# Sending one row of attention weights through DRAM instead of TensorE, and splitting the last block's feed-forward in two

## The chip, the cores and the metric

The kernel runs on one core of a Trainium2 chip, all in float32. The metric is device time in microseconds: the median of three runs, and beside it one profiled execution, from which all durations are taken. The engines are TensorE (PE; its weight loads are PEld), VectorE (DVE), ScalarE (ACT), GpSimd (POOL) and SyncE (SP), which here issues every DMA.

## The reference, cut to what matters

The input is x of shape (2, 4096, 256). First comes a recurrent mixing layer (a scan over 4096 tokens, then a group norm and a projection), added to x. Then come two layers of local attention and a gated feed-forward:

```
h = shift_token(x)                    # second half of the channels comes from the token before
q, k, v = split(h @ wqkv)             # 8 heads of 64
q, k = rotary(l2norm(q) * qs), rotary(l2norm(k) * ks)
# windows of 128 queries; keys: this window and the one before
mask = (i < j) | (i > j + 128)        # each query sees itself and the 128 tokens before it
o = softmax(q k^T * 8, masked) @ v
x = x + o @ wo
h = layernorm(shift_token(x)) * lg + lb
a, g = split(h @ w1 + b1)             # 682 each
x = x + (a * gelu(g)) @ w2 + b2
```

So each query sees 129 keys: 128 that can be laid out in 128 columns, and one more, the last key of the window before.

## The kernel before, in words

The work of the attention and feed-forward is cut into windows of 128 tokens, numbered n = 0 to 127, and blocks of four windows (512 tokens, number k): 2 sequences x 2 layers x 8 blocks. The recurrence of the first sequence runs ahead of them; that of the second runs beside the first windows.

A window with neighbours packs its 256 scores into 129 columns. Column 0 is the last key of the window before; columns 1 to 128 are the keys of this window, and where a query may not see its own window's key (a later one), the column holds the key of the window before that stands one place lower. Thus `pr[n]` is a tile of 128 queries x 8 heads x 129 weights. Column 0 is added onto column 1. `transpose_p(n, s)` transposes columns 1 to 128 of four heads each on TensorE into `ppt`, a PSUM bank. It copies them to `pT`, and multiplies them with the mask `backs` into `pB`, which keeps only the weights of keys of the window before. The mask leaves row 0 of `pB` empty, and column 0 of `pr`, turned into a row for each head, belongs there. In the kernel before, a ninth transposition (128 x 8 in, 8 x 128 out) brings this column to PSUM, a copy brings it to the small tile `last`, and a DMA writes `last` as row 0 of `pB`:

```
            pt = bank([P, W])
            nc.tensor.transpose(pt[:HEADS, :], pr[:, :, 0], ident)
            last = tile_of([P, W], "last", 2)[:HEADS]
            either(last, pt[:HEADS, :])
            nc.sync.dma_start(out=pBs[n][0:1], in_=last)
```

`values(n)` multiplies `pT` with the window's values `vt` and `pB` with `dv`, the difference between the values one window back and these (`vr`, the old values moved down by one row by DMA, minus `vt`, on POOL). It stands in one piece with `scores(n + 1)`, right behind its matmuls. Four of 128 windows start a sequence and have no window before (`lone`), so `pB` is made 124 times. There is one `pB` buffer.

After attention, `output` adds the projection by `wo` to x. `shift` moves half of the channels by one token with DMAs (tile `h`), and `normed` normalizes `h`. Before, `transpose_h(k)` transposes all four windows of a block when the last is there, and the feed-forward of the block follows over the next windows, in tiles of 512 tokens. `hidden` is one matmul pair over 128 columns of `w1`; `gate` and `remainders` copy gate tiles out of PSUM; `gelus` runs GELU over them as one unbroken piece on ScalarE; `value` multiplies the other half in; `down_ends` and `down` multiply by `w2`, one window at a time, and store. `fill(n, i)` places these steps into the windows that come after. For the last block no windows come after, and its feed-forward stands alone at the end.

No order is written by hand. Every call is only recorded, with a row (`plan.at`) as its priority; `order()` then simulates engines with fixed costs from `cost()` and puts out each engine's instructions in the order of planned starts. Among what can start first on an engine, the lowest row goes first. `either` lets the planner choose between ScalarE and VectorE for a copy. A DMA is planned to land `LAND` = 2500 ns plus its passes after its issue. PSUM has eight banks, which the planner hands out. All instructions are thus issued from line 524 (518 and 520 for scaling), so groups are told apart by their tiles. SP issues in order: when one DMA waits, those behind it wait too.

Of the kernel before, what the change touches and what calls it, by code (L numbers as in the profile page):

```python
# [15 lines left out]
P = 128  # L16
# [5 lines left out]
NM = 6  # L22
# [38 lines left out]
LEAN = 700  # L61
SLACK = 1.06
LOAD = 1283
LAND = 2500
TURN = {"row": 195, "col": 95, "full": 199}
SETS = {AF.Exp: 1, AF.Tanh: 1, AF.Gelu: 2, AF.Ln: 3}
# [15 lines left out]
class View:  # L82
# [51 lines left out]
    def to_broadcast(self, shape):  # L134
        return View(
            self.place,
            self.rows,
            np.broadcast_to(self.idx, shape[1:]),
            [*self.chain, ("to_broadcast", (shape,), {})],
        )  # L140

    def bitcast(self, dtype):
        return View(self.place, self.rows, self.idx, [*self.chain, ("bitcast", (dtype,), {})])
# [37 lines left out]
class Plan:  # L181
# [39 lines left out]
    def dram(self, shape, name):  # L221
        place = Place(int(np.prod(shape[1:])))
        place.outer = True
        place.real = self.dram_pool.tile([P, place.size], F32, tag=name, name=name)
        return self.view(place, 0, shape)

    def at(self, row):
# [74 lines left out]
    def cost(self, o):  # L302

        views = [*o.outs, *o.ins]
        n = max([v.idx.size for v in views] or [1])
        psum = any(v.place.psum for v in views)
        inside = sum(v.idx.size == n and not v.place.psum for v in o.ins)
        o.set, o.lock, o.half, o.passes, name, hold = None, False, "full", 0, o.name, None
        if o.eng == "tensor":
            trans = name == "transpose"  # L310
            left = o.args[1]
            move = o.args[2] if len(o.args) > 2 else o.args[1]
            cols = max(move.idx.size, left.idx.size) if not trans else P
            o.step = (1 if trans else 2) * (cols / 1.2 + (2 if cols >= 256 else 3))
            if not trans and left.shape[0] <= 64:
                o.half = "row"
            elif not trans and left.idx.size <= 64:
                o.half = "col"
            if o.half != "full":
                o.step /= 2  # L320
            o.time = o.step + 150
        elif o.eng == "vector":
            d = 150 + 1.04 * n
            if name == "tensor_tensor_reduce":
                d = 240 + 1.04 * n
            elif name == "tensor_tensor_scan":
                d, o.lock = 203 + 2.1 * n, True
            elif name == "scalar_tensor_tensor":
                d, o.lock = 200 + 1.05 * n, inside > 1
            elif name == "tensor_tensor":  # L330
                o.lock = inside > 1
            elif name == "tensor_scalar":
                d, o.lock = 155 + (1.27 if psum else 0.98) * n, not psum and n > 16
            elif name == "tensor_copy" and not psum:
                d, o.lock = 230 + 0.45 * n, n > 16
            elif name == "bn_aggr":
                d = 172
            elif name == "reciprocal":
                d = 147 + 4 * n
            o.step, o.time = max(d - 85, 60), d  # L340
        elif o.eng in ("scalar", "either"):
            d = (160 if psum else 195) + 0.83 * n
            if name == "scaled":
                d = 305 + 0.76 * n
            elif name == "activation":
                o.set = SETS.get(o.args[2])
                if o.args[2] == AF.Identity:
                    d = 365 + 0.87 * n
                elif isinstance(o.kw.get("bias"), View):
                    d += 85  # L350
            o.step, o.time = d - 100, d
            if "accum_out" in o.kw:
                o.time = d + 200
        elif o.eng == "gpsimd":
            o.lock = name != "memset"
            if name == "tensor_tensor":
                d = 430 + 156 * n if ALU.pow in o.args else 140 + 2.22 * n
            elif name == "tensor_scalar":
                d = 230 + 1.12 * n
            else:  # L360
                d = (100 if name == "memset" else 187) + 0.98 * n
            o.step, o.time = d, d
            hold = d if n > 64 else 100
        else:
            v = min(views, key=lambda v: v.shape[0] * v.idx.size)
            size = 4 * v.shape[0] * v.idx.size
            rows = max(v.shape[0] if v.shape[0] > 1 else v.shape[1] for v in views)
            ways = max(k for k in range(1, 17) if rows % k == 0)
            o.passes = size / 170 if ways == 16 else size / (25 * ways)
            inner = len(views) == 2 and not any(v.place.outer for v in views)  # L370
            o.step = 370 if not inner else 580 if ways in (1, 16) else 800
            o.time = LAND + o.passes
        o.hold = hold or o.time
# [154 lines left out]
def kernel(ctx: ExitStack, tc: tile.TileContext, a: dict, out: bass.AP):  # L528
# [581 lines left out]
    def softmax(n, g):  # L1110
# [42 lines left out]
        for m in range(2):  # L1153
            ph = prs[n][:, h0 + 2 * m, off:]
            nc.either.scaled(ph, ph, sums[:, m : m + 1])

    def transpose_p(n, s):


# [14 lines left out]
            ALU.mult,  # L1174
        )
        if s:
            pt = bank([P, W])
            nc.tensor.transpose(pt[:HEADS, :], pr[:, :, 0], ident)
            last = tile_of([P, W], "last", 2)[:HEADS]
            either(last, pt[:HEADS, :])  # L1180
            nc.sync.dma_start(out=pBs[n][0:1], in_=last)

    def values(n):

# [56 lines left out]
            nc.gpsimd.tensor_tensor(x[:, w, :], x[:, w, :], x1s[k][:, w, :], ALU.add)  # L1241
            plan.at(row)

    def transpose_h(k):
        l = blocks[k][0]
        h = hs.pop(k)
        hT = hTs[k] = tile_of([P, 2, T], "hT")
        for i in range(2):
            pt = bank([P, T])
            for w in range(NW):  # L1250
                nc.tensor.transpose(
                    pt[:, w * P : (w + 1) * P], h[:, w, i * P : (i + 1) * P], ident
                )
            g, bb = lnp[:, l, 0, i : i + 1], lnp[:, l, 1, i : i + 1]
            if i == 0:
                nc.scalar.activation(hT[:, i, :], pt, AF.Identity, bias=bb, scale=g)
            else:
                nc.vector.tensor_scalar(hT[:, i, :], pt, g, bb, ALU.mult, ALU.add)

    def hidden(k, c0, cols):  # L1260
        pm = bank([P, T])
        for i in range(2):
            nc.tensor.matmul(
                pm[:cols], w1[:, i, c0 : c0 + cols], hTs[k][:, i, :], start=(i == 0), stop=(i == 1)
            )
        return pm

    def gate(k, m):
        either(hm[:, m, :], hidden(k, m * P, P))

    def remainders(k):
        pm = hidden(k, G_LAST * P, HS)
        rems[k] = tile_of([P, NW // 2, P], "rem")
        for odd in range(2):
            rows = slice(64 * odd, 64 * odd + HR)
            nc.scalar.copy(ends[rows], of_half(pm[64:HS], odd))
            either(rems[k][rows], of_half(pm[:HR], odd))

    def of_half(t, odd):

        return t.rearrange("p (w two t) -> p w two t", two=2, t=P)[:, :, odd, :]

    def gelus(k):
        l = blocks[k][0]
        with piece():
            for m in range(NM - 1):
                g = hm[:, m, :]
                nc.scalar.activation(g, g, AF.Gelu, bias=b1[:, l, 1, m : m + 1])
            for odd in range(2):
                rows = slice(64 * odd, 64 * odd + HR)  # L1290
                g = ends[rows]
                nc.scalar.activation(g, g, AF.Gelu, bias=b1[rows, l, 1, NM - 1 : NM])

    def value(k, m):
        l = blocks[k][0]
        plan.early = k == NK - 1
        if m < NM - 1:
            src = hidden(k, G_LAST * P + HS + m * P, P)
            g = hm[:, m, :]
            nc.vector.scalar_tensor_tensor(g, src, b1[:, l, 0, m : m + 1], g, ALU.add, ALU.mult)  # L1300
        else:
            src = rems.pop(k)
            for odd in range(2):
                rows = slice(64 * odd, 64 * odd + HR)
                g = ends[rows]
                nc.vector.scalar_tensor_tensor(
                    g, src[rows], b1[rows, l, 0, m : m + 1], g, ALU.add, ALU.mult
                )
        plan.early = False

# [27 lines left out]
    def fill(n, i):  # L1338
# [4 lines left out]
            down(k, 2 * s)  # L1343
            down(k, 2 * s + 1)
        k = n // NW - 1
        if not 0 <= k < NK:
            return
        if s == 1:
            gate(k, i)
# [7 lines left out]
        elif s == 3 and i < 3:  # L1357
            value(k, i + 2)
            if i == 2:
                value(k, 5)  # L1360

# [80 lines left out]
    norms(0)  # L1444
    cosines(0)
    rotated(0)
    for n in range(NN + 6):
        k, w = divmod(n, NW)
        here, ahead, behind = n < NN, n + 1 < NN, 0 < n <= NN
        plan.at(n)  # L1450
# [44 lines left out]
        if behind:  # L1495
            output(n - 1)
            shift(n - 1)
            if here and n % (NB * NW) == 0:
                weights(n // (NB * NW) % L, "o")
        if w == 1 and 0 < k <= NK:  # L1500
            transpose_h(k - 1)
        if w == 2 and k + 1 < NK:
            transpose_x(k + 1)
# [17 lines left out]
        fill(n, 3)  # L1521
        if w < 2 and NW < n < NN and (n - NW - w) % (NB * NW) == 0:
            weights(n // (NB * NW) % L, "12"[w])
    with tc.manual_schedule():
        plan.give()

# [78 lines left out]
```

## Time and profile before

| | us |
|---|---|
| median of 3 runs | 2972.16 (2969.49 to 2972.76) |
| profiled execution, time | 2970.99 |
| profiled execution, span from first to last instruction | 2969.2 |
| TensorE busy | 2945.0 |
| VectorE busy | 2250.9 |
| ScalarE busy | 2018.8 |
| GpSimd busy | 1449.3 |
| DMA, share of 16 engines | 20.9% |

Busy time is the union of an engine's instructions. The durations of matmuls overlap in TensorE's pipeline, so what one costs is read from the distance between starts and not from its duration. A float32 matmul appears as two records in the trace, a transposition as one. "us to landing" of a DMA runs from its issue on SP until the last of its engines has counted up its semaphore.

### The profile page before, as it was taken

The numbers are of one execution on the slowest core, as the hardware profiler recorded it, in microseconds if no ns is written. First come the engines' busy times: TensorE is split into PE (matmuls) and PEld (weight loads), VectorE is DVE, ScalarE is ACT, GpSimd is POOL, SyncE is SP. The second block draws the span as 40 slices with busy tenths as digits, with TensorE's granted clock in tenths as the row PEclk, the third lists the DMA queues.
The fourth block names the chain that finished last, engine by engine and source line by source line (L and its number), as shares of the span: only waits on it lengthen the run. The fifth ranks groups of instructions, "written<-read, shape, count | busy, mean of one in ns | idle before, by whom it ended". The sixth has DMA issues, their size and how long they took to land.

```text
span 2969.2 us, 48964 instructions
## 1 busy us (share of the span) xinstructions
PE 2945.0 (99%) x15548; PEld 1913.7 (64%) x15548; DVE 2250.9 (76%) x5088; ACT 2018.8 (68%) x5359; POOL 1449.3 (49%) x1705
## 2 busy tenths in 40 slices
PE   9999999999999999999999999999999999999998
PEld 4476766666666666666666666666666666666665
DVE  7889999998866788786777677777676676767673
ACT  7887787778666777776666666666666666666663
POOL 2226654555554555445555444545454554555550
PEclk9999999999999999999999999999999999999999
DMA  2324322221121211111122221111112211111110
GB/s 85 114 78 133 115 69 87 75 82 53 60 65 54 83 48 53 56 59 55 52 77 79 74 68 48 61 58 61 55 44 70 70 57 49 58 55 54 47 40 27
DMA packets 185227, 195.09 MB, mean 66 GB/s; under 512 B 27812, under 2 KB 148484, under 8 KB 184456
## 3 DMA queue, kind: packets, MB, share of 16 engines
q1 hardware_dynamic: 184968, 191.96, 20.9%
q8 instruction: 123, 2.02, 0.3%
q14 instruction: 136, 1.11, 0.1%
HBM read 85.46 MB, written 39.85 MB: 42 GB/s over the span
## 4 chain that ended last, share of the span: by engine, by line
PE 92%; DVE 3%; ACT 3%; issue 1%; POOL 0%; DMA 0%; SPq 0%; POOLq 0%; ACTq 0%; DVEq 0%
PE bank L524 92%; ACT pr L524 1%; ACT L524 1%; DVE arena L524 1%; DVE bank L524 0%; ACT pr L520 0%; DVE sq L524 0%; DVE qk L524 0%; DVE h L524 0%; DVE nmx L524 0%; DVE hm L524 0%; DVE pB L524 0%; ACT arena L524 0%; ACT oT L524 0%; ACT hm L524 0%
## 5 line engine op out<-in xcount | busy, mean ns | idle before, releaser
L524 PE MATMUL bank<-wqkv,xT 128*128 128x512 f32 x1536 | 723.8, 596 | 0.5 <-ACT xT L524 0.5
L524 PE MATMUL bank<-hT,w 128*128 128x512 f32 (+1 forms) x1408 | 652.2, 595 | 0.0
L524 POOL TENSOR_TENSOR t<-qk,tab 128x256 f32<-128x256 f32 x512 | 383.6, 768 | 471.2 <-ACT qk L524 362.3
L524 ACT ACTIVATE pr<-bank,nmx 128x129 f32<-128x129 f32 (+1 forms) x1024 | 369.5, 379 | 147.8 <-DVE nmx L524 146.4
L524 PEld LDWEIGHTS bank<-hT,w 128*128 128x128 f32 (+1 forms) x1408 | 254.8, 189 | 260.9 <-issue 247.3
L524 PEld LDWEIGHTS bank<-wqkv,xT 128*128 128x128 f32 x1536 | 266.4, 191 | 210.9 <-issue 207.3
L524 POOL TENSOR_TENSOR rn<-rn,mhalf 128x16 f32<-128x16 f32 x128 | 391.7, 3060 | 8.8
L520 ACT ACTIVATE pr<-pr,sums 128x129 f32<-128x129 f32 (+1 forms) x948 | 334.1, 418 | 40.7 <-DVE pr L524 39.9
L524 DVE COPY_PREDICATED bank<-packs,bank 128x254 f32<-128x254 int32 x496 | 186.4, 420 | 229.8 <-PE bank L524 229.7
L524 PE MATMUL bank<-w,hm 128*128 128x256 f32 x1280 | 294.0, 381 | 0.0
L524 POOL TENSOR_TENSOR dv<-vr,vt 128x512 f32<-128x512 f32 x124 | 165.4, 1334 | 201.2 <-PE bank L524 188.1
L524 PEld LDWEIGHTS bank<-w,hm 128*128 128x128 f32 x1280 | 239.7, 190 | 35.0 <-issue 4.2
L524 ACT COPY qk<-bank 128x512 f32<-128x512 f32 x225 | 132.3, 588 | 170.5 <-PE bank L524 164.0
L524 PE MATMUL bank<-kT,qT 64*128 64x256 f32 (+1 forms) x2048 | 246.1, 380 | 0.4 <-ACT kT L524 0.4
L524 PE MATMUL bank<-wo,oT 128*128 128x256 f32 x1024 | 243.0, 380 | 1.4 <-ACT oT L524 1.3
L524 PEld LDWEIGHTS bank<-wo,oT 128*128 128x128 f32 x1024 | 193.4, 190 | 70.5 <-ACT oT L524 22.6
L524 PEld LDWEIGHTS bank<-kT,qT 64*128 64x128 f32 x2048 | 190.4, 187 | 68.8 <-issue 36.0
L524 DVE TENSOR_TENSOR pB<-bank,backs 128x512 f32<-128x512 f32 x248 | 170.0, 686 | 83.5 <-PE bank L524 56.7
L524 ACT ACTIVATION_READ_ACCUMULATOR pr<-bank,nmx 128x1 f32 x1024 | 221.8, 217 | 0.0
L524 ACT COPY hm<-bank 128x512 f32<-128x512 f32 x170 | 99.8, 587 | 174.1 <-PE bank L524 173.1
L524 PEld LDWEIGHTS bank<-mats,pr 128*128 128x128 f32 x1148 | 134.9, 135 | 115.7 <-issue 73.2
L524 PE MATMUL bank<-pT,vt 128*64 128x128 f32 x2048 | 203.3, 279 | 0.0
(159 smaller groups left out, 5625.3 us busy)
## 6 DMA issues: line engine op xcount, KB each, us to landing
vr<-vt SPq DMA_DIRECT2D x124, 224.0 KB
tab<-in_c_rot_dram SPq DMA_DIRECT2D x128, 128.0 KB
kT<-kT SPq DMA_DIRECT2D x64, 256.0 KB
z<-zd SPq DMA_DIRECT2D x16, 512.0 KB
x<-in_x_dram SPq DMA_DIRECT2D x16, 512.0 KB
x1d<-x SPq DMA_DIRECT2D x16, 512.0 KB
x<-x1d SPq DMA_DIRECT2D x16, 512.0 KB
h<-x SPq DMA_DIRECT2D x128, 64.0 KB
```

Source lines behind the costliest of these rows:

```text
L520: self.nc.scalar.activation(dst, src, AF.Copy, scale=scale)
L524: getattr(getattr(self.nc, o.eng), name)(*args, **kw)
```

## The change

First, column 0 of `pr` goes out as one DMA into a DRAM row, transposed by the access pattern (8 heads x 128 queries, one value at a time), and a second DMA brings the row back as row 0 of `pB`. Two DRAM rows take turns. The ninth transposition, its copy and `last` are gone. The planner gets a cost for such a transfer, `SINGLES` = 1500 ns of passes.

Second, the feed-forward of the last block is taken out of the loop over windows and done by a function of its own in two groups: each has two windows of 128 tokens, with all steps from `transpose_h` to `down`. Its matmuls of `hidden` have 256 columns instead of 512, so there are twice as many. The first group has a lower row number (128) than the second (130). The other blocks keep tiles of 512.

```diff
+SINGLES = 1500
...
+            if any(v.idx.size > 1 and v.idx.ravel()[1] != v.idx.ravel()[0] + 1 for v in views):
+                o.passes = SINGLES
...
+    fronts = [plan.dram([1, HEADS * W], f"front_{i}") for i in range(2)]
+
     def transpose_p(n, s):
...
         if s:
-            pt = bank([P, W])
-            nc.tensor.transpose(pt[:HEADS, :], pr[:, :, 0], ident)
-            last = tile_of([P, W], "last", 2)[:HEADS]
-            either(last, pt[:HEADS, :])
-            nc.sync.dma_start(out=pBs[n][0:1], in_=last)
+            row = fronts[n % 2]
+            nc.sync.dma_start(out=row.seen("o (h q) -> (o q) h", h=HEADS), in_=pr[:, :, 0])
+            nc.sync.dma_start(out=pBs[n][0:1].rearrange("o h q -> o (h q)"), in_=row)
...
-    def transpose_h(k):
+    def transpose_h(k, w0=0, w1=NW):
...
-    def hidden(k, c0, cols):
-        pm = bank([P, T])
+    def hidden(k, c0, cols, ts):
+        pm = bank([P, ts.stop - ts.start])
         for i in range(2):
             nc.tensor.matmul(
-                pm[:cols], w1[:, i, c0 : c0 + cols], hTs[k][:, i, :], start=(i == 0), stop=(i == 1)
+                pm[:cols], w1[:, i, c0 : c0 + cols], hTs[k][:, i, ts], start=(i == 0), stop=(i == 1)
             )
...
         k = n // NW - 1
-        if not 0 <= k < NK:
+        if not 0 <= k < NK - 1:
             return
...
+    def last_block():
+
+        k = NK - 1
+        for w in (0, 2):
+            plan.at(NN + w)
+            ts = slice(w * P, (w + 2) * P)
+            transpose_h(k, w, w + 2)
+            for m in range(NM - 1):
+                gate(k, m, ts)
+            remainders(k, ts)
+            gelus(k, ts)
+            for m in range(NM):
+                value(k, m, ts)
+            down_ends(NN + NW + w // 2)
+            down(k, w)
+            down(k, w + 1)
...
-    for n in range(NN + 6):
+    for n in range(NN + 2):
...
-        if w == 1 and 0 < k <= NK:
+        if w == 1 and 0 < k < NK:
             transpose_h(k - 1)
...
+    last_block()
```

More of the change, by code (lines that the diff above doesn't have):

```diff
@@ L140, in to_broadcast, with seen @@
         )
+    def seen(self, pattern, **sizes):
+        return View(self.place, self.rows, self.idx, [*self.chain, ("rearrange", (pattern,), sizes)])
     def bitcast(self, dtype):
@@ L223, in dram @@
         place.outer = True
-        place.real = self.dram_pool.tile([P, place.size], F32, tag=name, name=name)
+        place.real = self.dram_pool.tile([shape[0], place.size], F32, tag=name, name=name)
         return self.view(place, 0, shape)
@@ L1242, in shift @@
             plan.at(row)
-    def transpose_h(k):
+    def transpose_h(k, w0=0, w1=NW):
         l = blocks[k][0]
-        h = hs.pop(k)
-        hT = hTs[k] = tile_of([P, 2, T], "hT")
+        h = hs[k]
+        if w0 == 0:
+            hTs[k] = tile_of([P, 2, T], "hT")
+        hT = hTs[k][:, :, w0 * P : w1 * P]
         for i in range(2):
-            pt = bank([P, T])
-            for w in range(NW):
+            pt = bank([P, (w1 - w0) * P])
+            for w in range(w0, w1):
                 nc.tensor.transpose(
-                    pt[:, w * P : (w + 1) * P], h[:, w, i * P : (i + 1) * P], ident
+                    pt[:, (w - w0) * P : (w - w0 + 1) * P], h[:, w, i * P : (i + 1) * P], ident
                 )
@@ L1258, in transpose_h, with gate, halves, remainders @@
                 nc.vector.tensor_scalar(hT[:, i, :], pt, g, bb, ALU.mult, ALU.add)
-    def hidden(k, c0, cols):
-        pm = bank([P, T])
+    def hidden(k, c0, cols, ts):
+        pm = bank([P, ts.stop - ts.start])
         for i in range(2):
             nc.tensor.matmul(
-                pm[:cols], w1[:, i, c0 : c0 + cols], hTs[k][:, i, :], start=(i == 0), stop=(i == 1)
+                pm[:cols], w1[:, i, c0 : c0 + cols], hTs[k][:, i, ts], start=(i == 0), stop=(i == 1)
             )
         return pm
[L1268 to L1277, printed above, removed]
+    ALL = slice(0, T)
+    def gate(k, m, ts=ALL):
+        either(hm[:, m, ts], hidden(k, m * P, P, ts))
+    def halves(ts):
+        pairs = slice(ts.start // (2 * P), ts.stop // (2 * P))
+        return [(odd, slice(64 * odd, 64 * odd + HR), pairs) for odd in range(2)]
+    def remainders(k, ts=ALL):
+        pm = hidden(k, G_LAST * P, HS, ts)
+        if ts.start == 0:
+            rems[k] = tile_of([P, NW // 2, P], "rem")
+        for odd, rows, pairs in halves(ts):
+            nc.scalar.copy(ends[rows, pairs], of_half(pm[64:HS], odd))
+            either(rems[k][rows, pairs], of_half(pm[:HR], odd))
     def of_half(t, odd):
         return t.rearrange("p (w two t) -> p w two t", two=2, t=P)[:, :, odd, :]
-    def gelus(k):
+    def gelus(k, ts=ALL):
         l = blocks[k][0]
@@ L1286, in gelus, with value @@
             for m in range(NM - 1):
-                g = hm[:, m, :]
+                g = hm[:, m, ts]
                 nc.scalar.activation(g, g, AF.Gelu, bias=b1[:, l, 1, m : m + 1])
-            for odd in range(2):
-                rows = slice(64 * odd, 64 * odd + HR)
-                g = ends[rows]
+            for odd, rows, pairs in halves(ts):
+                g = ends[rows, pairs]
                 nc.scalar.activation(g, g, AF.Gelu, bias=b1[rows, l, 1, NM - 1 : NM])
-    def value(k, m):
+    def value(k, m, ts=ALL):
         l = blocks[k][0]
@@ L1297, in value @@
         if m < NM - 1:
-            src = hidden(k, G_LAST * P + HS + m * P, P)
-            g = hm[:, m, :]
+            src = hidden(k, G_LAST * P + HS + m * P, P, ts)
+            g = hm[:, m, ts]
             nc.vector.scalar_tensor_tensor(g, src, b1[:, l, 0, m : m + 1], g, ALU.add, ALU.mult)
         else:
[L1302 to L1305, printed above, removed]
+            for odd, rows, pairs in halves(ts):
+                g = ends[rows, pairs]
                 nc.vector.scalar_tensor_tensor(
-                    g, src[rows], b1[rows, l, 0, m : m + 1], g, ALU.add, ALU.mult
+                    g, rems[k][rows, pairs], b1[rows, l, 0, m : m + 1], g, ALU.add, ALU.mult
                 )
```

## The prediction

> **What bounds the kernel now.** I read the page's busy time first, then its chain, then TensorE's idle time by stretch, then the groups of the instructions that the change touches, and last the timeline of one window and of the end.
>
> ```profile
> PE 2945.0 (99%) x15548; PEld 1913.7 (64%) x15548; DVE 2250.9 (76%) x5088; ACT 2018.8 (68%) x5359; POOL 1449.3 (49%) x1705
> PE 92%; DVE 3%; ACT 3%; issue 1%; POOL 0%; DMA 0%; SPq 0%; POOLq 0%; ACTq 0%; DVEq 0%
> ```
>
> TensorE is busy 99% of the span, and 92% of the chain that ended last is its own work. The windows view says where the idle 24 us are:
>
> ```profile
> 300.00:600.00 300.00, 299.23 (x1657) 201.37 (x1654) 280.55 (x638) 234.98 (x615) 166.80 (x215) 1.00 0.27 85
> 2100.00:2400.00 300.00, 299.86 (x1628) 194.95 (x1626) 205.73 (x474) 188.16 (x534) 152.99 (x167) 1.00 0.21 64
> 2930.00:2935.00 5.00, 0.57 (x3) 0.57 (x4) 1.02 (x3) 0.06 (x1) 1.49 (x3) 0.93 0.08 28
> 2935.00:2940.00 5.00, 4.98 (x12) 2.36 (x11) 0.81 (x1) 1.31 (x2) 0.00 (x0) 0.73 0.01 3
> ```
>
> (The columns after the stretch are the busy us of PE, PEld, DVE, ACT and POOL, then the granted clock, the DMA share, GB/s.) Between 300 and 2890 us TensorE is busy 2586.45 of 2590, so there only less TensorE work shortens the kernel. At the end there is a real hole: 4.4 us idle in 2930 to 2935, after which the granted clock averages 0.73 for 5 us.
>
> The groups that the first edit removes:
>
> ```profile
> L524 PE MATMUL bank<-mats,pr 128*8 128x128 f32 x124 | 33.8, 273 | 0.0
> L524 ACT COPY last<-bank x97: 247/249/255, 272.9 to 2915.9; 8x128 f32<-8x128 f32 x97
> L524 DVE COPY last<-bank x27: 269/269/273, 355.7 to 2819.3; 8x128 f32<-8x128 f32 x27
> L524 SPq DMA_DIRECT2D pB<-last x124: 662/693/736, 273.8 to 2916.8; - x124
> ```
>
> And the timeline, one ninth transposition among its neighbours, then the end:
>
> ```profile
> 2900.13 0.27 PE L524 MATMUL bank<-mats,pr 128*8 128x128 f32 x1
> 2900.24 1.88 PE L524 MATMUL bank<-hT,w 128*128 128x512 f32 x4
> ...
> 2929.86 0.34 SPq L524
> 2930.25 1.96 DMA h<-x
> ...
> 2934.43 1.33 PE bank L524 x5
> ```
>
> The next matmul starts 0.11 us after the transposition, not 0.27: durations overlap in the pipeline. The last three lines are of the chain of waits: the last window's shifted rows are issued only behind an output store (2929.86), land 1.96 us later, and the normalized tile lets TensorE go on at 2934.43.
>
> **The change part by part. Sum against the profiled execution: span 2969.2 us, 2970.99 in all, 1.2 us under the median 2972.16.**
>
> *Removed: 124 transpositions.* How much each is worth is the main choice. The row's duration gives 124 x 0.273 = 33.8 us. The Trainium skill (TensorE: Matmul & The Clock Gate, Part 4: PE-mode transpose) also has about 275 ns for a transposition inside a kernel, and says that access latency is most of it; by that figure I would take 34 us off. But the sum must be made of steps: 0.11 us from start to start here, and eight query/key transpositions take 2901.96 to 2902.83, 0.109 each. So 124 x 0.109 = **13.5 us**, all of it in the stretch where TensorE is never idle. The changed program's instruction order has the same number of changes between full-array and half-array matmuls, so none of that is gained or lost.
>
> *Removed: the copies of the row out of PSUM.* 97 x 0.249 + 27 x 0.269 = 31.4 us of ScalarE and VectorE. Both have idle time (68% and 76% busy), so zero. From above: TensorE's whole idle time from 300 to 2890 is 3.5 us, and freeing a PSUM bank for some us per window can at most shorten that and small stalls that the busy time hides. From below: freed time reorders other work, which can also hurt. I take 0, ends -4 and +6 (gain).
>
> *Moved to DMA: per window a scatter of 128 x 8 single values into DRAM, then one 4 KB row back, in place of `pB<-last`.* Three things.
> (a) The landing. No row of before moves single values. The trace's completion events give, from issue to landing (medians): `pB<-last` 1.81 us (8 rows of 512 B), `kT<-kT` 2.71 (512 rows of 512 B, 32 for each of 16 engines), a 128 KB store `out_dram<-x` 1.86, a 128 KB load `tab<-in_c_rot_dram` 2.13. From the first two, (2.71 - 1.81)/32 = 28 ns for each 512-byte run. The scatter has 1024 runs, 64 for each engine: at most 64 x 28 = 1.8 us above 1.86, so 3.7; at least, with the 9 ns that a 4-byte packet takes in the packet records, 0.6 above, 2.4. Here a rule speaks against the change: the Trainium skill (DMA: Bandwidth & Descriptors, Rules for kernel authors) says that a last dimension with a stride becomes one descriptor per element, and warns off transposing by a rearranged access pattern, with a factor of 19. Nineteen times 1.81 is 34 us; with 13 us available in a window, 21 x 124 = 2600 us would be lost. I do not take it: the rows show that most of 1.81 us is fixed and that descriptors spread over engines, so only the 1024 count applies. I take 2.9 for the scatter and 2.1 for the row back: with wake-ups 5.2 us, against 0.25 + 1.81 + the transposition's place in the queue before.
> (b) Who waits for it. `values` of this window, which TensorE runs right behind the next window's scores. In the changed instruction order I summed steps (0.428 us per 512-column pass, half for 256, 0.109 per transposition, about 0.2 at each change of array half) from the eighth transposition to the first `pB` matmul: minimum 5.3, lowest 5% 7.1, median 8.8. The last weights are ready before that transposition: in the trace of before, from the last normalization of `pr` to the first `pB` matmul, median 13.1, lowest 5% 8.8, minimum 5.8. So 5.2 us fits in every window: **0 us**. The cover is the 8.8 us of feed-forward, projection and score matmuls; without it each late us would cost 124 us.
> (c) SP's queue. One more issue per window, 124 x 0.35 (a DRAM transfer such as `tab`) to 0.70 (`kT`): 43 to 87 us of a queue that already waits 654.6 us for POOL's `dv` alone. The second transfer waits for the first to land; in the changed order 1 to 9 other transfers stand between them (`vr`, `h`, `tab` mostly), each 0.35 to 0.85 us, so SP stands at most about 2 us in the 19 windows with only one between. Behind it then are `kT<-kT` (42 windows; the next scores wait for it) and `vr<-vt` (39; `dv` on POOL). Both are also late-bound on ScalarE's `kT` copy or on POOL, as before. I take 0, ends +3 and -10. Packets: 124 x 1024 x about 10 ns over 16 engines is 80 us each, 2.7% of the span, on top of 20.9%: hidden.
>
> *The last block in two groups.* Work is equal: 44 passes of 512 columns become 88 of 256, 0.214 each. Before, from the last `wo` matmul (ends 2927.2) to the last matmul (2966.2) is 39.0 us. In the changed order the first group's transpositions and four gates (0.4 + 3.4 us) stand before the last window's `values`, and 2.1 + 6.0 + 2.1 = 10.3 us of work (two `down`, seven hidden tiles) stand between the last `wo` matmul and the second group's transpositions. The last window's shift and norm takes 2927.2 to 2934.4 = 7.2 us, so the hole closes: +4.7, and with it the slow clock, 5 us at 0.73 = +1.35. What is late next: the first group's `down_ends` waits for the whole run of its gelus. After its remainder tile ScalarE needs two copies (0.4 each), a table load of 1.28, five gelus of half length (about 0.42) and two short ones, VectorE two products: about 6 us, over 3.4 us of TensorE work (one hidden tile, one `down`, four transpositions): -2.5. The second group's own gelus end with its last hidden tile, as before. Net of these and half-length evictions (about +1): **4.5 us**, ends 1.5 and 7.
>
> Sum: 13.5 + 4.5 = 18.0; 2971.0 - 18.0 = 2953.0 in the profile, and against the median **2954.2**.
>
> **Rivals.**
> *Rescheduling takes part of it back* (14%). The order is planned from estimated times, and each window shifts. For it: half-array turns and short stalls already hide some 0.6 us per window inside TensorE's busy time, as a window of 21.2 us holds 20.6 us of steps. Against: the steps between dependent instructions are nearly as in before. If it costs 0.05 us per window, 6 us, and the end gives 1.5: 2972.2 - 13.5 + 6 - 1.5 = 2963; with more, 2966, range 2960 to 2975.
> *The detour is late, and `values` waits* (11%): slower. Place: the first `pB` matmul of a window. Summing what is missing over the 124 windows with the second transfer and wake-ups at 2.2 us: nothing for a scatter of up to 4 us, 7 us at 5.0, 20 at 5.5, 33 at 6.0, 89 at 7.0. It decides from 5.5 us, or from some 1.5 us later as weights are ready before the eighth transposition. For it: no row shows 4-byte writes to DRAM, and SP issues in order. At 6.0 with no such credit: 2972.2 - 18 + 33 = 2987; up to 3043.
> *The freed bank and copies help too* (5%): 2954 - 10 = 2944.
> *The end does not split*: excluded by the changed instruction order, which shows the 256-column tiles before the last `values`.
>
> **How the numbers follow.** The main case, 70%, is 2954 with its own range 2946 to 2962 (the ends above: copies, SP, end). The range 2945 to 2968 adds over half of the first rival and part of the third. Left out: the slower case and the outer parts of the others, 2 in 10. A measurement of this kernel can tell 0.2%, 5.9 us, from no change: faster is below 2966.2. Faster: 0.70 + half of 0.14 + 0.05 = 0.82; same 0.07; slower 0.11.
>
> **What would show it.** Right: no `128*8` group, TensorE busy less by 13 to 17 us, no entry of PE waiting for DMA `pB<-front`, ScalarE's copies fewer by about 24 us, some 127,000 more packets, and at the end no TensorE hole over 3 us and a clock near 1.00. Wrong: PE or PEld waiting for `pB<-front`; SP waiting over 3 us for `front<-pr` in the median window; a landing of the scatter over 5 us; TensorE busy unchanged though the transpositions are gone (then stalls took their place); idle time in front of `w,ends` at the end of over 4 us.

## The result, and the profile after

The changed kernel takes 3551.26 us (median of 4 runs, 3546.63 to 3557.81) against 2971.36: a ratio of 1.1954, interval 1.1939 to 1.1968. It is 580 us slower, where 18 us faster was forecast. First the busy time of the page after, with the granted clock in its 40 slices and the DMA share:

```profile
span 3544.8 us, 48728 instructions
PE 3112.4 (88%) x15468; PEld 2014.1 (57%) x15468; DVE 2240.4 (63%) x5068; ACT 2013.8 (57%) x5281; POOL 1425.3 (40%) x1705
PEclk9999999989999999999999999999999999999999
DMA packets 312450, 195.59 MB, mean 55 GB/s; under 512 B 155904, under 2 KB 275584, under 8 KB 311680
q1 hardware_dynamic: 312192, 192.48, 24.4%
```

TensorE is now idle 3544.8 - 3112.4 = 432 us, before 24. Its busy time has grown by 167 us although 124 transpositions are gone. The mean granted clock of the execution is 0.948 instead of 0.998, and 5% of 3112 us is 156. So the loss is holes in TensorE's work, some 408 us, and slower running around them, the rest. There are 127,000 more DMA packets, as forecast, and the DMA engines' recorded share went from 20.9% to 24.4%: by this count they look mostly idle.

The windows view shows the same for the middle of the run (columns as in the prediction):

```profile
300.00:600.00 300.00, 259.99 (x1355) 176.41 (x1355) 223.82 (x502) 188.60 (x483) 138.98 (x175) 0.95 0.39 76
2100.00:2400.00 300.00, 270.45 (x1410) 176.25 (x1408) 190.18 (x441) 157.27 (x433) 121.09 (x148) 0.97 0.23 48
```

Who waited for a DMA, first before, then after (us in total, times, longest):

```profile
POOL x L524 <- DMA h<-x: 141.8, 41, 11.9
DVE st L524 <- DMA h<-x: 30.8, 27, 2.6
POOL tab L524 <- DMA tab<-in_c_rot_dram: 21.4, 21, 2.5
```

```profile
DVE st L531 <- DMA h<-x: 442.9, 72, 9.5
POOL x L531 <- DMA h<-x: 382.7, 42, 15.0
POOL tab L531 <- DMA tab<-in_c_rot_dram: 315.7, 53, 13.1
PE bank L531 <- DMA pB<-front: 177.1, 66, 5.5
```

The last line is the wait that a rival of the prediction named: `values` waits for the row. But the three above it are larger, and they wait for transfers that the change does not touch: the shifted half of `h`, from SBUF to SBUF, and the rotary table. The timeline of SP shows one window:

```profile
2120.61 0.49 SPq L531 DMA_DIRECT2D front<-pr  x1
2121.15 0.58 SPq L531 DMA_DIRECT2D vr<-vt  x1
2121.83 0.52 SPq L531 DMA_DIRECT2D xmd<-x  x1
2122.45 0.38 SPq L531 DMA_DIRECT2D tab<-in_c_rot_dram  x1
2132.22 0.24 SPq L531 DMA_DIRECT2D pB<-front  x1
```

The scatter is issued at 2120.61, and the second transfer can go only at 2132.22: the landing took over 11 us. In the waits of SP's queue:

```profile
SPq L531 <- DMA front<-pr: 852.4, 115, 10.7
```

By the trace's completion events the scatter lands 10.7 us after its issue (median; 5% to 95%: 9.3 to 11.6), where 2.9 was taken. The packet records are done with it long before: nearly all of its 4-byte packets lie between 0.8 and 2.1 us after the issue, 7 to 9 ns each. And of `h<-x`, 5% now land after more than 10.4 us, before 3.0.

### The profile page after: what moved, and what is told of

Read it like the earlier page. It is cut to its first block, busy times and chain, and to the rows that moved or that the text cites. A ratio compares the mean times of both kernels' runs of the same rounds, so it can differ in the third digit from the quotient of the medians.

```text
span 3544.8 us, 48728 instructions
## 1 busy us (share of the span) xinstructions
PE 3112.4 (88%) x15468; PEld 2014.1 (57%) x15468; DVE 2240.4 (63%) x5068; ACT 2013.8 (57%) x5281; POOL 1425.3 (40%) x1705
## 3 DMA queue, kind: packets, MB, share of 16 engines
q1 hardware_dynamic: 312192, 192.48, 24.4%
## 5 line engine op out<-in xcount | busy, mean ns | idle before, releaser
L531 PE MATMUL bank<-wqkv,xT 128*128 128x512 f32 x1536 | 741.0, 609 | 0.5 <-ACT xT L531 0.5
L531 PE MATMUL bank<-hT,w 128*128 128x512 f32 (+3 forms) x1452 | 655.3, 585 | 0.4 <-ACT hT L531 0.4
L531 DVE BATCH_NORM_STATS2 st<-h 128x6 f32<-128x256 f32 x128 | 54.4, 425 | 608.1 <-DMA h<-x 442.9
L531 PE MATMUL bank<-pB,dv 128*64 128x128 f32 x1984 | 244.8, 323 | 209.4 <-DMA pB<-front 177.1
L531 PE MATMUL bank<-kT,qT 64*128 64x256 f32 (+1 forms) x2048 | 277.2, 408 | 86.7 <-ACT qT L531 63.9
L531 PEld LDWEIGHTS bank<-pB,dv 128*64 128x64 f32 x1984 | 160.1, 165 | 226.8 <-POOL rs L531 94.3
L531 POOL TENSOR_TENSOR tab<-tab,qks 128x256 f32<-128x256 f32 x128 | 116.3, 909 | 354.7 <-DMA tab<-in_c_rot_dram 315.7
L531 PE MATMUL bank<-pT,vt 128*64 128x128 f32 x2048 | 244.7, 317 | 6.7 <-DVE hm L531 5.3
L531 POOL TENSOR_TENSOR x<-x,x 128x256 f32<-128x256 f32 x64 | 48.1, 751 | 489.5 <-DMA h<-x 382.7
L531 ACT COPY pT<-bank 128x512 f32<-128x512 f32 x195 | 115.3, 591 | 214.9 <-DVE pB L531 126.7
```

The costliest lines, as they stand in the source:

```text
L531: getattr(getattr(self.nc, o.eng), name)(*args, **kw)
```

## The experiments

Two questions. Is the loss the wait for the row (theory A), or does the scatter hold up the other transfers (theory B)? And why does it land so late? All kernels start from the changed one and have its split last block, so split_only is the base for the edits of the scatter. Medians of the kernel before beside these runs were 2971.1 to 2971.7 us.

**The split alone.** The five lines of the ninth transposition put back in place of the detour:

```diff
-    fronts = [plan.dram([1, HEADS * W], f"front_{i}") for i in range(2)]
...
-            row = fronts[n % 2]
-            nc.sync.dma_start(out=row.seen("o (h q) -> (o q) h", h=HEADS), in_=pr[:, :, 0])
-            nc.sync.dma_start(out=pBs[n][0:1].rearrange("o h q -> o (h q)"), in_=row)
+            pt = bank([P, W])
+            nc.tensor.transpose(pt[:HEADS, :], pr[:, :, 0], ident)
+            last = tile_of([P, W], "last", 2)[:HEADS]
+            either(last, pt[:HEADS, :])
+            nc.sync.dma_start(out=pBs[n][0:1], in_=last)
```

> The last block in two groups, with the ninth transposition, its copy and the DMA from last kept as before. Theory: the whole loss comes from the detour through DRAM, and the split gives what the prediction gave it, 1.5 to 7 us: 2964 to 2970 us, likeliest 2967, with no hole of TensorE over 3 us at the end. Rival: the split itself does harm, by smaller tiles or a wait for the gelus: 2972 us or more.

Measured: 2965.53 us, ratio 0.9981 (0.9973 to 0.9989). The split gives 5.5 us, and all of the loss is the detour's. The end of its windows view and its timeline:

```profile
2930.00:2935.00 5.00, 5.00 (x25) 4.33 (x24) 1.02 (x3) 3.43 (x9) 1.50 (x3) 1.00 0.01 3
2935.00:2940.00 5.00, 5.00 (x24) 3.92 (x23) 3.12 (x8) 2.76 (x7) 0.00 (x0) 1.00 0.08 27
```

```profile
2927.17 8.80 PE L531 MATMUL bank<-hT,w 128*128 128x256 f32 x40
2928.20 0.85 SPq L531 DMA_DIRECT2D h<-x  x1
...
2943.34 0.60 PE L531 MATMUL bank<-mats,h 128*128 128x128 f32 x4
2944.37 9.76 PE L531 MATMUL bank<-hT,w 128*128 128x256 f32 x44 [0.44 <-ACT hT L531]
```

While the last window's shift lands, TensorE works on the first group. The hole of 4.4 us and the clock of 0.73 behind it are gone.

**The scatter issued, but nobody waits for its row.** As split_only, and besides

```diff
+    fronts = [plan.dram([1, HEADS * W], f"front_{i}") for i in range(2)]
...
+            row = fronts[n % 2]
+            nc.sync.dma_start(out=row.seen("o (h q) -> (o q) h", h=HEADS), in_=pr[:, :, 0])
```

> As split_only, and in each of the 124 windows the scatter of single values into DRAM is issued as well, but nothing reads its row: the weights take the ninth transposition as before. Theory A, the loss is the wait for the row (SP waits for the first landing, values for the second): 2967 to 2985 us, though the scatter still lands after 10 to 11 us. Theory B, the pending writes hold up every other transfer on the same DMA engines: most of the loss stays, over 3150 us, with h, tab and xmd landing after up to 10 us. A mixture lies between, and its place says the shares.

Measured: 3527.42 us, ratio 1.1873 (1.1854 to 1.1891); the scatter lands after 10.3 us. So theory B: the mere presence of the writes costs 3527.4 - 2965.5 = 562 us. Reading the row and waiting for it add little: 3551.3 against 3527.4, 24 us, or some 35 as the change saves the transpositions (11 us, below). The two costs overlap, since what waits for `h` meanwhile cannot also lose by the row. Its waits:

```profile
DVE st L531 <- DMA h<-x: 499.0, 80, 9.8
POOL x L531 <- DMA h<-x: 333.7, 39, 15.8
POOL tab L531 <- DMA tab<-in_c_rot_dram: 225.1, 45, 12.4
PE bank L531 <- DMA pB<-last: 96.7, 46, 6.3
```

The last one is telling: the old little transfer `pB<-last`, SBUF to SBUF, 1.81 us before, lands after 7.1 us (median), since it is issued in the scatter's shadow.

**The planner told of the late landing.**

```diff
-SINGLES = 1500
+SINGLES = 7500
```

> The changed kernel with SINGLES = 7500, so that the planner counts on the scatter's landing after 10.0 us instead of 4.0. Theory A: the order now puts other work of SP and TensorE into the wait, and most of the loss goes: 2970 to 3060 us. Theory B, or a chain too long to be filled: over 3200 us.

Measured: 3298.13 us, ratio 1.1101 (1.1086 to 1.1117), over the limit that was set for theory B. The planner's own model also delays later DMAs behind such a transfer, and it moves work so that 253 us come back. More than half of the loss stays: it is not only a plan with wrong times.

**Is it the ring?** The scatter of idle_scatter issued from ScalarE's DMA queue, in rings of its own:

```diff
+            if name == "dma_start" and o.passes == SINGLES:
+                self.nc.scalar.dma_start(*args, **kw)
+                continue
```

> As idle_scatter, but the scatter is issued from ScalarE's DMA queue instead of SP's, so it stands in rings of its own on the same 16 DMA engines. Theory H1, the others are held because they stand behind the scatter in SP's rings: h, tab and last land in about 2 us, and the time is 2965 to 3050 us. Theory H2, the engines, or the way to DRAM, are held: the others still land after up to 10 us, 3300 to 3600 us.

Measured: 3492.5 us, ratio 1.1755 (1.169 to 1.182). What stands on SP's rings still lands late (`pB<-last` 5.9 us in the median, 5% of `h<-x` after more than 10.6), as in its waits:

```profile
DVE st L534 <- DMA h<-x: 509.8, 89, 9.0
POOL x L534 <- DMA h<-x: 341.9, 37, 14.7
```

The scatter's own queue in the DMA view of this run (packets, MB, share of the engines' time) shows how little time its packets take on record:

```profile
q10 hardware_dynamic: 128960, 0.52, 1.7%
```

So H2: it is not the place in the queue, and transfers that never touch DRAM are held too.

What is held can be seen in part in the traces. The smallest piece of `h<-x` (16 packets of 32 bytes, SBUF to SBUF) is easily told from the other packets. Where it follows the scatter within 6 us, its last packet ends 1.39 us after its issue, as everywhere else; but its landing, by the completion events, comes after 8.9 us in idle_scatter and 9.8 in idle_act (medians of 14 and 23) instead of 1.7. And every `h<-x` that was issued while the scatter was pending landed after the scatter, 129 of 129 in idle_scatter and 155 of 155 in idle_act, half of them within 0.5 us of it. So a small transfer's data is on record in time, and its completion waits until the scatter's writes are in. Of larger transfers the packets are late as well: in the window of the changed kernel shown above, packets of 1 KB are spread out until 2131.5, single ones taking up to 3 us where about 0.05 is usual. Why the completions wait, no run here tells.

**Why late: the values moved apart.** As idle_scatter, with 512 bytes for each value. (`picked` rearranges the real access pattern and takes one element.)

```diff
-    fronts = [plan.dram([1, HEADS * W], f"front_{i}") for i in range(2)]
+    fronts = [plan.dram([1, HEADS * W * P], f"front_{i}") for i in range(2)]
...
+            cells = row.picked("o (h q x) -> (o q) h x", (slice(None), slice(None), 0), h=HEADS, x=P)
+            nc.sync.dma_start(out=cells, in_=pr[:, :, 0])
```

> As idle_scatter (3527 us), but each of the 1024 single values goes to a 512-byte line of its own in DRAM, where they shared eight lines. Theory W1, each short write to DRAM has a price of its own, (10.3 - 1.9) us over 1024 = 8.2 ns: the landing stays at 9 to 11 us and the time at 3400 to 3600. Theory W2, writes to the same lines queue behind each other: landing 2.5 to 4 us and 2965 to 3020 us.

Measured: 2963.28 us, ratio 0.9974 (0.9963 to 0.9985), no loss at all beside split_only. The scatter lands after 2.7 us. It is the same 1024 writes of 4 bytes from the same 16 engines: W1 is out, and W2 holds in its main point: what is slow is not the number of short writes but that they go 4 bytes apart into the same few stretches of DRAM.

**Half of the values.** Only heads 0 to 3, four stretches of 512 bytes with 128 writes each:

```diff
+            row = fronts[n % 2][:, : HEADS // 2 * W]
+            nc.sync.dma_start(
+                out=row.seen("o (h q) -> (o q) h", h=HEADS // 2), in_=pr[:, : HEADS // 2, 0]
+            )
```

> As idle_scatter, but only four of the eight heads are scattered: 512 single values in four lines, still 32 for each engine less 0, with nobody reading them. W1 and W2 with all lines written side by side: landing 1.9 + 4.2 = 6.1 us, and the loss over split_only (562 us) more than halves, since part of a 4 us hold is covered: 2980 to 3250 us. If the hold is a fixed time after any scatter instead: landing 10 us and 3500 us.

Measured: 3164.36 us, ratio 1.0651 (1.062 to 1.0681), in the range; but the landing takes 9.2 us, not 6.1. With half the writes the time to land hardly shrinks. What stays the same is how densely a stretch is written, and that fits stretches that are filled side by side. My number for the landing was W1's and was wrong. The smaller loss, 199 us over split_only instead of 562, cannot be laid to the number of writes: this scatter does not wait for the last four heads and stands elsewhere in the order. `pB<-last` is issued 11.5 us behind it (median; 4.2 in idle_scatter) and lands in 1.8 us, while more of `h<-x` is late (median 7.4 us against 1.95). What each place is worth is open.

**Fewer and longer writes to the same 4 KB.** GpSimd first gathers the values into a 128 x 8 tile, and 32-byte runs are written, untransposed:

```diff
+            col = tile_of([P, HEADS], "col", 2)
+            nc.gpsimd.tensor_copy(col, pr[:, :, 0])
+            nc.sync.dma_start(out=row.seen("o (q h) -> (o q) h", h=HEADS), in_=col)
```

> As idle_scatter, but GpSimd first gathers the eight values of each query into a 128 x 8 tile (about 0.2 us per window), and the transfer writes 128 runs of 32 bytes in the same 4 KB of DRAM, not transposed. Both W1 and W2 go by the number of writes: landing 1.9 + 128 x 8.2 ns = 3.0 us, 2965 to 2985 us. If it goes by the bytes or the place in DRAM: landing 10 us.

Measured: 2964.6 us, ratio 0.9979 (0.997 to 0.9987); landing 1.5 us. So the place in DRAM and the bytes alone do not make a transfer late; many single values close together do.

**The same values, not transposed.** Single values again, in the order in which they come. The thought behind it: if each DMA engine takes neighbouring queries (the traces do not tell which engine writes which value), few engines then write into the same 512 bytes.

```diff
+            nc.sync.dma_start(out=row.seen("o (q h) -> (o q) h", h=HEADS), in_=pr[:, :, 0])
```

> As idle_scatter, but the single values are written in the order in which they come, query by query: the same 1024 writes of 4 bytes to the same 4 KB and the same 128 for each 512 bytes[...]. If the number of writes to a line decides, landing 9 to 11 us and 3400 to 3600 us. If it is engines that meet in a line: landing 2 to 4 us and 2962 to 2985 us.

Measured: 3206.83 us, ratio 1.0792 (1.077 to 1.0814), landing 7.9 us. It lies between the two forecasts. Single values close together are slow without the transposed order too. That engines which meet in one stretch make it slower still is possible but not shown, as the order of the writes changed with it.

One thing the runs leave open is how long the stretch is in which writes get into each other's way. The landings of idle_scatter and idle_half would fit any length up to the 2 KB of idle_half, and the "line" of 512 bytes in the forecasts is a guess. The fast runs say only that single values 64 bytes apart, or runs of 32 bytes, do not suffer. So no price per write follows.

**The change as it was meant, with the values apart.** The full detour with spacings of 512 and of 64 bytes (the edit for 512; for 64 the three 128s are 16):

```diff
-    fronts = [plan.dram([1, HEADS * W], f"front_{i}") for i in range(2)]
+    fronts = [plan.dram([1, HEADS * W * 128], f"front_{i}") for i in range(2)]
...
+            every = slice(None)
+            cells = row.picked("o (h q x) -> (o q) h x", (every, every, 0), h=HEADS, x=128)
+            nc.sync.dma_start(out=cells, in_=pr[:, :, 0])
+            cells = row.picked("o (i x) -> o i x", (every, every, 0), x=128)
+            nc.sync.dma_start(out=pBs[n][0:1].rearrange("o h q -> o (h q)"), in_=cells)
```

> The change as it was meant, with nine TensorE transpositions down to eight and the row read back from DRAM, but each single value has a 512-byte line of its own, so the read back is 1024 single values too. If shared lines were the whole fault, the scatter lands in about 2.7 us, the row in 2.5 to 4, values does not wait, and the time is that of heads_direct (2954) with six issues of SP fewer per window: 2948 to 2958 us. If gathering single values from DRAM is slow as well, or the added wait matters, over 2975.

> As spread_512, but the values stand 64 bytes apart: eight in each 512 bytes instead of 128. If a line takes one write after the other, at (10.3 - 1.9) us / 128 = 66 ns each, eight of them add 0.5 us at most: landing under 3.3 us and 2948 to 2962 us. If any sharing of 512 bytes among engines is the fault: landing near 10 us and over 3300 us.

Measured: 3096.05 us, ratio 1.0419 (1.0401 to 1.0437), and 3075.03 us, ratio 1.0341 (1.0317 to 1.0366). The scatter does land after 2.8 us in both, so eight values in 512 bytes do no harm, as forecast. My forecast of the time missed in both: reading 1024 single values back takes 7.2 us, not 2.5 to 4, and the plan counted on 2.5. With 2.8 + 7.2 = 10.0 us for the detour, `values` waits:

```profile
PE bank L535: 105.2, 52
```

(from the view of tile `front` of spread_512: who waited for it, us and times). This is the prediction's rival in a nearly clean form: `h<-x` lands as before (median 1.93 us, 95% under 3.2), but `kT<-kT`, next in the queue, is late (median 4.3). A detour of 10 us costs about 120 to 140 us over the next kernel, which makes eight transpositions as well.

**No DRAM.** Eight transfers per window straight into row 0 of `pB`, planned with `SINGLES` = 200 each:

```diff
-SINGLES = 1500
+SINGLES = 200
...
+            for h in range(HEADS):
+                nc.sync.dma_start(out=pBs[n][0:1, h, :], in_=pr[:, h, 0:1])
```

> No DRAM: eight DMAs per window, one for each head, each of 128 single values straight from pr into row 0 of pB in SBUF (SINGLES = 200 for each). Theory C, what is slow is single values written to DRAM: each lands in 2 to 3 us, and the time is 2950 to 2990 us, where SP's eight issues of about 0.5 us are the only cost. Rival D, single values are slow wherever they go: landings over 5 us and over 3200 us in all.

Measured: 2954.44 us, ratio 0.9945 (0.9931 to 0.9958), faster than both kernels. Of its page, and of its view of tile `pB`:

```profile
PE 2930.7 (99%) x15468; PEld 1910.5 (65%) x15468; DVE 2232.1 (76%) x5056; ACT 2014.9 (68%) x5292; POOL 1448.9 (49%) x1705
L531 SPq DMA_DIRECT2D pB<-pr x992: 468/540/1577, 271.0 to 2907.9; - x199
DMA to landing us min/median/max: 1.9/2.0/5.3
```

The same 4-byte writes, 128 per transfer, land in 2.0 us in SBUF. SP issues 868 transfers more, and nothing on TensorE waits for them. TensorE is busy 2930.7 us, 11.1 less than in split_only (2941.8), and the time is 11.1 us less.

## Why the prediction was wrong, point by point

- **What bounds the kernel** held. heads_direct shows it: TensorE work taken away comes off the time one for one.
- **The ninth transposition by steps, 13.5 us,** held nearly: 11.1 measured. By durations (273 ns on the trace, and about 275 in the Trainium skill, TensorE: Matmul & The Clock Gate, Part 4: PE-mode transpose) 34 us would have been expected; the step was the right measure.
- **The split, 4.5 us,** held: 5.5 measured, hole and clock as described. With both, heads_direct came to 2954.4 us, where 2954.2 was forecast for the change; that it is so near is partly luck, as the two misses lean opposite ways.
- **Step (a), the landing of the scatter at 2.9 us, failed.** The price per run came from `kT<-kT` and from packet records, so it counted what a DMA engine spends on a run. For 1024 values that stand apart it is right (2.7 and 2.8 measured). It left out where the values go: 4 bytes apart, 128 of them into each 512 bytes. The packet records end some 2 us after the issue; the landing came after 10.7. The sentence "descriptors spread over engines, so only the 1024 count applies" was the wrong reason to put the warning of the Trainium skill (DMA: Bandwidth & Descriptors, Rules for kernel authors: no transposing by a rearranged access pattern) aside. The factor of 19 there compares with the chip's own DMA transpose, which no run here has, so to put it on the 1.81 us of `pB<-last` was a mistake of its own: the landing grew to 10.7, 5.9 times. The same page (Specifications) says that transfers below 512 bytes are done by read-modify-write; no run here shows the mechanism, and single values that stood apart were not slow.
- **Step (c), packets at 2.7% of the engines' time, "hidden",** failed worse, and no rival had it. The scatter's own packets took no more than forecast: 1.7% of the span in idle_act, where they have a queue to themselves. But that is time on record, not time for which others are held. The rise to 24.4% of a longer span in the changed kernel (865 us for each engine, before 621) is mostly other transfers' packets that take longer. And the largest part of the loss, 562 us, comes with no one waiting for the row.
- **The slower rival** named the place that did wait (177 us at the first `pB` matmul) and what decides it, the scatter's landing. Its price stopped at a landing of 7.0 us, and so its worst time at 3043. And it priced the wait alone: reading the row added 24 to 35 us, while what the scatter does to other transfers, which costs 562, stood in no rival.

## What to carry to other kernels

A DMA has a length that no busy share shows, from the last packet to the completion, and other transfers on its engines may be held until it ends. When a transfer's pattern is new to a kernel, ask how close together its writes fall in DRAM, and measure its landing with nobody waiting before anything is built on it. Eight transfers of single values within SBUF, which land in 2.0 us, did what the detour was meant to do.

## What the runs showed of the hardware that I had not expected

- 1024 single 4-byte writes side by side in 4 KB of DRAM land after 10.3 to 10.7 us (7.9 in their natural order), and 512 of them in 2 KB after 9.2; spaced by 64 or 512 bytes, 1024 of them land in 2.7 to 2.8 us.
- While such writes are pending, other transfers, SBUF to SBUF too and from another queue, land some 8 us late. A small one has its packets on record in time, and only its completion waits for the scatter's.
- Reading 1024 spaced single values from DRAM into one partition takes 7.2 us, against 2.0 for one run of 4 KB.
